# Splitting layer 0's score maxima into two halves on GpSimd instead of VectorE

## The chip, the cores and the metric

The kernel runs on one core of a Trainium2 chip. A core has five engines with instruction queues of their own: TensorE (PE; its weight loads are listed as PEld), VectorE (DVE), ScalarE (ACT), GpSimd (POOL) and SyncE (SP), which issues transfers. Each queue is worked off in its fixed order, and engines wait for each other by semaphores. The metric is the device time of one execution in microseconds (us). One profiled execution comes with it, whose span is counted from the first to the last instruction.

## The reference

Two cross-attention layers follow each other, for 8 batches of 100 queries of width 512 and 722 context rows each. Cut to what matters:

```python
# layer 0: 16 heads of width 32
Q = layer_norm(x) @ wq + bq;  K = layer_norm(ctx) @ wk + bk;  V = layer_norm(ctx) @ wv + bv
scores = einsum('bqhd,bkhd->bhqk', Q, K) / sqrt(32)
out = einsum('bhqk,bkhd->bqhd', softmax(scores), V) @ wo + bo
x = x + out
x = x + gelu(layer_norm(x) @ w1 + b1) @ w2 + b2
# layer 1: 16 heads of width 64, on the x of layer 0 and the same context
out = softmax(x @ Wq (x scale) @ (ctx @ Wk).T) @ (ctx @ Wv) @ Wfc + x
out = layer_norm(out) * gamma + beta
```

All inputs and the output are float32.

## The kernel before

Matrix products run on float16 operands. To keep accuracy, every float32 operand is split into a high half (the value rounded to float16) and a low half (the rest, also float16), and a product is made of the three terms of `TERMS`: high x high, high x low, low x high.

The work is cut in 24 units, numbered `u`: units 0 to 7 are the batches of layer 0 with 16 heads each, units 8 to 23 are half batches of layer 1 with 8 heads each. The outer loop at the end of `xattn_kernel` goes over units and heads and calls `step(u, h)`. After each step it takes items from a list (`fill`): projections of keys and values for the next unit, the normalisation and transposition of later context rows (`prep0`, `prep1`), the scaling and splitting of weights (`block`), the feed-forward part (`ffn`), output projections (`post0`, `post1`), each with an estimated cost.

A head of layer 0 goes through these stages.

- `scores`: two matmuls make the 100x722 scores `S` in PSUM, and VectorE reduces them to `nm`, the negated maximum of each of the 100 rows.
- `negated`: `nm` is split into a high and a low half, which are put in columns 96 and 97 of a 100x98 float16 tile, one of a ring of four (`NM`); its other columns are zero. In the high half the value is divided by `MS` = 2048.
- `negated_T`: a matmul with the identity turns that tile, so that the two halves become rows 96 and 97 of a result in the PSUM tile `NZB`, and ScalarE copies them into rows 96 and 97 of the head's queries `q`.
- `front0`: six matmuls make the transposed scores `ST` from 98 rows. Rows 96 and 97 of the keys tile hold the constants `MS` and `LS`, so that the negated maximum is added by the matmul itself. ScalarE takes the exponential into `p` and casts it into the high half of `pt`, and GpSimd makes the low half with two subtractions of 128x300.
- `head_back`: twelve matmuls multiply `pt` with the values into `O`.

`step(u, h)` calls `scores`, `negated` and `negated_T` for head h and then `front0` for an earlier head, of two steps before in layer 0. `S` and `ST` share a PSUM ring of two tiles. In layer 1 `front1` gives `nm` to ScalarE as a bias, and `negated` and `negated_T` aren't called.

The program is not run in the order in which it is written. Each engine's order is laid down by a planner ahead of the run (`TC_KW = dict(schedule_with_timeline_sim=True)`), from estimated durations and priorities; the instructions of a step are raised in priority (`tc.high_priority`). Only in the first steps are the orders of the queues those of the program (`nc.in_order`), with the calls written out by hand in an order of their own. The profile names one line (L40) for nearly all instructions, as they pass through a recording helper (`Engine`), so that groups are told apart by the tiles that they write and read.

The tiles that matter here: `nm` is the maximum and also the split tile, `nzb` the PSUM tile of the turned halves (some projections use it too), `QS` the queries, `S` and `ST` the scores, `p` and `pt` the probabilities, `V` and `KN` the values and keys, `pp` the PSUM tiles of the projections, `nat` a context tile in natural layout, `hl` the two halves of one, `xs` a tile of rows of x.

Of the kernel before, what the change touches and what calls it, by code (L numbers as in the profile page):

```python
# [12 lines left out]
ALU = mybir.AluOpType  # L13
AX = mybir.AxisListType

B, SQ, SK, E, FF = 8, 100, 722, 512, 2048
# [9 lines left out]
MS = 2.0 ** 11  # L26
# [28 lines left out]
def xattn_kernel(  # L55
# [4 lines left out]
    nc = Core(tc)  # L60
# [49 lines left out]
    def ring(name, tiles):  # L110
        i = counters.get(name, 0)
        counters[name] = i + 1
        return tiles[i % len(tiles)]
# [603 lines left out]

    def negated(nm):
        nz = ring("nm", NM)
        nc.vector.tensor_scalar(nz[:, 96:97], nm[:SQ], 1.0 / MS, None, ALU.mult)  # L720
        nc.vector.tensor_scalar(nz[:, 97:98], nz[:, 96:97], -MS, nm[:SQ], ALU.mult, ALU.add)
        return nz

    def negated_T(u, h, nz):
# [732 lines left out]
    def step(u=None, h=None):  # L1457

        with tc.high_priority(offset=80 if u == LAST or u is None and len(pending) and pending[0][0] >= LAST - 1 else 105):
            new = None  # L1460
            if u is not None:
                S, nm = scores(u, h)
                new = (u, h, S, negated(nm) if u < B else nm)
                if u < B:
                    negated_T(u, h, new[3])
            if len(stages) >= (2 if u is not None and u < B else 1):
                v, g, S_, nm_ = stages.pop(0)
                pending.append((v, g, front0(v, g, nm_) if v < B else front1(v, g, S_, nm_)))
                used.add((v, g))
            if new:  # L1470
                stages.append(new)
# [84 lines left out]
```

## Time and profile before

| what | value |
|---|---|
| time, median of 3 runs | 1536.39 us (1535.56 to 1539.84) |
| profiled execution, its own time | 1540.27 us |
| profiled execution, span | 1538.5 us |
| mean granted TensorE clock | 0.966 |
| busy TensorE (matmul) | 1385.8 us, 90% |
| busy VectorE | 1015.8 us, 66% |
| busy ScalarE | 813.6 us, 53% |
| busy GpSimd | 580.4 us, 38% |

Busy shares are averages over stages with different limits: layer 0's heads run in the first 660 us, with the preparation of all weights beside them, and layer 1's from then on. A line of the waits view reads: engine and tile that waited, the engine and tile that ended the wait, total us, number of waits, longest. A line of the groups view reads: engine, operation, out<-in, partitions x elements and type, count, busy us, mean ns of one, then the idle time of the engine ahead of them and what ended it.

### The profile page before, as it was taken

To read this page: it belongs to the slowest core of one execution; us is meant where nothing else is said; L and a number is where in the kernel's file an instruction comes from. 1 tells how busy PE (TensorE), PEld (TensorE's weight loads), DVE (VectorE), ACT (ScalarE), POOL (GpSimd) and SP (SyncE) were. 2 spreads that over 40 slices of the span, in tenths; PEclk is the share of its full clock that TensorE was granted. 3 is DMA by queue.
4 is the path that set the end of the run, shared out by engine and by line. 5 is a ranking of instruction groups with operands and counts; after the bars stand their busy time and mean duration, and the time that the engine had idled before them with its cause. 6 is when DMAs were issued, how large, how long until landed. Compare 5 with 4: busy or idle time off the path is not lost. (4 is left out here: it accounts for less than half of the span.)

```text
span 1538.5 us, 33710 instructions
## 1 busy us (share of the span) xinstructions
PE 1385.8 (90%) x12586; PEld 985.0 (64%) x12586; DVE 1015.8 (66%) x2744; ACT 813.6 (53%) x1552; POOL 580.4 (38%) x572
## 2 busy tenths in 40 slices
PE   6888888897878999898999898999899999999996
PEld 5666666676657775566666566666566676566674
DVE  7787888888895676675456755556854555545555
ACT  4455767788865776654354343444343444334442
POOL 4145565665674453452123232122322222323341
PEclk9899999899979999999999999999999999999998
DMA  8567899998966565579577879687768867867684
GB/s 214 131 144 189 211 240 220 238 235 223 239 153 175 164 195 185 132 173 195 144 174 198 173 173 212 160 181 188 176 156 206 187 162 189 185 158 152 149 170 111
DMA packets 456660, 279.20 MB, mean 181 GB/s; under 512 B 348932, under 2 KB 387892, under 8 KB 456496
## 3 DMA queue, kind: packets, MB, share of 16 engines
q1 hardware_dynamic: 454352, 277.02, 74.3%
q8 instruction: 99, 1.62, 0.4%
q14 instruction: 65, 0.53, 0.1%
q10 hardware_dynamic: 2112, 0.01, 0.1%
q0 software_dynamic: 32, 0.01, 0.0%
HBM read 150.88 MB, written 35.30 MB: 121 GB/s over the span
## 5 line engine op out<-in xcount | busy, mean ns | idle before, releaser
L40 POOL TENSOR_TENSOR stage<-p,stage 100x722 f16<-100x722 f32 x124 | 194.1, 1570 | 477.1 <-DVE stage L40 242.3
L40 PE MATMUL pp<-wres,ctxT 128*128 128x256 f16 (+3 forms) x2004 | 335.3, 320 | 8.7 <-DVE KN L40 5.4
L40 PE MATMUL pp<-ctxT,wres 128*128 128x361 f16 x1836 | 326.2, 327 | 17.0 <-DVE V L40 6.3
L40 PEld LDWEIGHTS <-wres 128*128 128x128 f16 x2496 | 240.4, 100 | 144.3 <-issue 22.0
L40 PEld LDWEIGHTS <-ctxT 128*128 128x128 f16 (+1 forms) x2376 | 238.4, 103 | 141.7 <-issue 15.4
L40 DVE TENSOR_REDUCE nm<-S 100x1 f32<-100x722 f32 x256 | 229.9, 900 | 62.0 <-PE S L40 60.3
L40 POOL TENSOR_TENSOR pt<-p,pt 128x300 f16<-128x300 f32 x256 | 200.0, 804 | 180.2 <-ACT pt L40 100.1
L40 PE MATMUL O<-V,pt 128*128 128x64 f16 (+5 forms) x3840 | 201.5, 191 | 27.1 <-DMA pt<-stage 8.2
L40 PEld LDWEIGHTS <-pt 128*128 128x128 f16 (+1 forms) x3840 | 173.7, 99 | 69.2 <-issue 10.2
L40 PE MATMUL S<-ks,QS 128*100 128x361 f16 (+1 forms) x768 | 175.3, 327 | 26.1 <-DVE nm L40 10.8
L40 ACT ACTIVATE p<-S,nb,sig 100x722 f32<-100x722 f32 x128 | 121.8, 953 | 116.3 <-DVE nb L40 99.0
L40 DVE TENSOR_TENSOR V<-pp,V 128x256 f16<-128x256 f32 (+2 forms) x196 | 90.6, 463 | 106.9 <-ACT V L40 106.6
L40 ACT CAST V<-pp 128x256 f16<-128x256 f32 (+2 forms) x196 | 79.2, 407 | 152.7 <-PE pp L40 97.0
L40 PEld LDWEIGHTS <-QS 128*100 128x100 f16 (+1 forms) x768 | 88.5, 127 | 49.4 <-issue 23.6
L40 PEld LDWEIGHTS <-wst 128*128 128x128 f16 x1152 | 100.2, 99 | 13.8 <-DMA wst<-W1S 2.8
L40 ACT ACTIVATE p<-ST,sig 128x600 f32<-128x600 f32 x128 | 97.1, 758 | 13.8 <-PE ST L40 10.0
L40 ACT CAST KN<-pp 128x361 f16<-128x361 f32 x89 | 40.9, 460 | 104.1 <-PE pp L40 92.0
L40 ACT CAST pt<-p 128x600 f16<-128x600 f32 x128 | 88.1, 689 | 2.1
L40 DVE TENSOR_TENSOR KN<-pp,KN 128x361 f16<-128x361 f32 x89 | 47.2, 531 | 56.3 <-ACT KN L40 54.8
L40 PE MATMUL nzb<-ctxT,wres 128*128 128x361 f16 x468 | 81.7, 318 | 2.1 <-DVE sx L40 1.3
L40 PE MATMUL nzb<-wres,ctxT 128*128 128x512 f16 (+2 forms) x372 | 80.6, 366 | 0.2 <-DVE KN L40 0.2
L40 PE MATMUL ST<-QS,ks 98*128 98x100 f16 x768 | 61.0, 212 | 14.7 <-ACT p L40 9.5
(266 smaller groups left out, 2038.9 us busy)
## 6 DMA issues: line engine op xcount, KB each, us to landing
ks<-KN SPq DMA_DIRECT2D x256, 90.2 KB
nat<-in_ctx_dram SPq DMA_DIRECT2D x78, 256.0 KB
ks<-KD SPq DMA_DIRECT2D x96, 180.5 KB
wst<-W1S SPq DMA_DIRECT2D x64, 256.0 KB
wst<-W2S SPq DMA_DIRECT2D x64, 256.0 KB
wst<-WFS SPq DMA_DIRECT2D x48, 256.0 KB
KD<-KN SPq DMA_DIRECT2D x32, 361.0 KB
QS<-QD SPq DMA_DIRECT2D x85, 100.0 KB
```

Of the source, the lines that this page charges most:

```text
L40: r = f(*args, **kwargs)
```

## The change

The two instructions of `negated` are issued on GpSimd instead of VectorE. They are the same operations on the same 100x1 operands; the planner then lays down the orders of all queues anew.

```diff
     def negated(nm):
         nz = ring("nm", NM)
-        nc.vector.tensor_scalar(nz[:, 96:97], nm[:SQ], 1.0 / MS, None, ALU.mult)
-        nc.vector.tensor_scalar(nz[:, 97:98], nz[:, 96:97], -MS, nm[:SQ], ALU.mult, ALU.add)
+        nc.gpsimd.tensor_scalar(nz[:, 96:97], nm[:SQ], 1.0 / MS, None, ALU.mult)
+        nc.gpsimd.tensor_scalar(nz[:, 97:98], nz[:, 96:97], -MS, nm[:SQ], ALU.mult, ALU.add)
         return nz
```

## Prediction

> **What bounds the kernel now.** I read the windows view first, cut at the stretch in which layer 0's heads run (the first score maximum starts at 53.5 us, the last `negated` at 652.8 us). Columns: TensorE, its weight loads, VectorE, ScalarE, GpSimd, then granted clock, DMA share and GB/s.
>
> ```profile
> 55.00:660.00 605.00, 520.97 (x5360) 400.85 (x5359) 466.56 (x1440) 420.36 (x779) 316.79 (x367) 0.94 0.74 194
> ```
>
> TensorE is busy 521 of 605 us and stands still for 84. VectorE has 467 us of work, GpSimd 317, so GpSimd has 288 us free here. From 800 to 1538 us, where layer 1 runs and `negated` is not called, TensorE is busy 695 of 738 us: little to win there, and none of its instructions change. So the question is who ends the 84 us. The waits view of TensorE for the same stretch (us in total, times, longest):
>
> ```profile
> PE S L40 <- DVE nm L40: 10.8, 14, 1.3
> PE ST L40 <- ACT p L40: 9.5, 9, 2.9
> PE pp L40 <- DVE V L40: 7.0, 5, 2.5
> PE O L40 <- ACT pt L40: 6.9, 5, 2.9
> PE pp L40 <- DVE KN L40: 6.6, 7, 2.1
> PE nzb L40 <- DVE nm L40: 6.4, 6, 2.7
> ...
> PE ST L40 <- DVE nm L40: 4.3, 5, 1.5
> PE O L40 <- POOL pt L40: 4.0, 8, 0.8
> ```
>
> All lines that VectorE ends add up to 43.7 us (the five shown 35.1, nine smaller ones 8.6); those of ScalarE 29.8, of GpSimd 4.0. VectorE is thus the most frequent cause, but only half of the idle time. The view of the tile `nm` in this stretch prices what is moved (durations min/median/max in ns):
>
> ```profile
> L40 DVE TENSOR_SCALAR nm<-nm x127: 117/144/157, 56.2 to 652.6; 100x1 f16<-100x1 f32 x127
> L40 DVE TENSOR_SCALAR nm<-nm,nm x127: 177/206/218, 57.4 to 652.8; 100x1 f16<-100x1 f16 x127
> ```
>
> Last, the groups and waits of GpSimd there, which tell what the moved pair will be queued among:
>
> ```profile
> L40 POOL TENSOR_TENSOR pt<-p,pt 128x300 f16<-128x300 f32 x254 | 198.1, 802 | 180.2 <-ACT pt L40 100.1 <-PE nzb L40 22.2 <-PE ST L40 17.8
> ```
>
> GpSimd's main work is the low half of each head's probabilities, two instructions per head, and for 100 us it stands at the head of its queue waiting for ScalarE's cast of that tile (37 times, longest 11.4 us).
>
> **The change part by part.**
>
> *Off VectorE.* 128 heads x (144 + 206 ns) = 44.8 us, 9.6% of VectorE's 467. All that follows a pair in VectorE's queue can be earlier. What TensorE sees of it lies between 0 and 43.7 us (every wait that VectorE ends now). To place it, I took the instruction records: TensorE's gaps of over 0.1 us that end within 0.4 us after a VectorE instruction are 58 and 45.7 us long. From each I walked back through VectorE's queue to its last pause of over 0.12 us, counted the moved instructions in that run and shortened the gap by 175 ns for each, at most by the gap itself. The sum is 19.3 us. Example: the longest, 2.67 us at a `nzb` matmul, follows a run of 18.9 us with 8 moved instructions and shrinks by 1.4. I take 12 of the 19, because ScalarE ends 29.8 us of TensorE's idle time and is late next.
>
> *Onto GpSimd.* 128 x 2 small instructions. No GpSimd TENSOR_SCALAR of this shape is in the trace. Below, a memset of 128x1 takes 98 to 101 ns and one of 100x98 199 ns; above, extending the TENSOR_TENSOR rows to no columns (804 ns at 300, 1570 ns at 722, so 1.8 ns a column) leaves 260 ns, and a per-partition operand may add to it, so I put the upper end at 450 ns. I take 250, next to that intercept, since these instructions read and write as those do. The second one waits for the first: 0.05 us more, an estimate from the gaps of 0.03 to 0.04 us that VectorE shows between the two when nothing stands between. So 128 x 0.55 = 70 us (32 to 122 by the ends), and GpSimd goes from 317 to about 387 of 605 us, still the least loaded of the four.
>
> *Latency of one pair.* Now the pair is done on average 1.77 us after the maximum (0.74 until the first starts, 0.67 between them, because other VectorE work is interleaved, and the two durations). At the end of a maximum GpSimd's running instruction has on average 0.26 us left; with 0.1 to wake up and 0.55 of work the pair would be done after 0.9. TensorE loads `nz` 3.6 us after the maximum in the median (5% of heads under 1.4). Put in at that instant, 3 to 7 of 128 heads would be later than TensorE takes them now, by 1 to 3.4 us together: 2 us.
>
> *What waits behind it.* The new waits are for the maximum (VectorE) and for a free `nz` (TensorE). Queued behind are the `pt` subtractions and the `hl`, `whl` and `xs` work. 19 to 54 GpSimd instructions would be pushed, by 5 to 24 us in all. TensorE's second `O` matmul, first reader of the low half, starts 2.7 us in the median after the subtraction that it needs, under 0.4 us in a tenth of the heads. So about a tenth shows: 1 us.
>
> *What it waits behind.* GpSimd's order is fixed before the run by the planner's estimates. Where a pair stands behind a subtraction whose cast isn't there yet, it waits for work of earlier heads, and `negated_T` then holds TensorE. If every pair stood behind the next GpSimd instruction that hadn't started at the maximum's end, 50 of 128 would be later than now, by 81 us in all (67 to 102 by the ends of the price). I take one in 27, 3 us, since the planner knows both; this is the weakest number here.
>
> *The shared memory port.* The trace shows the two engines excluding each other. VectorE's normalisation, mostly 0.54 us, lasts 2.97 while GpSimd works without a break:
>
> ```profile
> 192.29 2.97 DVE L40 TENSOR_SCALAR nat<-nat,mv,rz 100x512 f32<-100x512 f32 x1
> ```
>
> The 45 of them take 516/540/2973 ns (min/median/max). With GpSimd's load up by 70 us in 605, 12% more of them meet a GpSimd instruction, 45 x 0.12 = 5, by up to 0.25 us each: 1 us, inside the rounding of the terms above. The Trainium skill (Perfetto Trace Analysis, Optimizing Scalar/DVE Operations) speaks against the change: moving work between VectorE and GpSimd may not help because they share a read port. Taken so strictly that GpSimd's new time came back on VectorE in full, it would leave 45 - 70 = -25 us, a loss; the row above shows the lock in full, but only some dozen of the 45 lasted longer than 0.6 us.
>
> *The sum.* -12 + 2 + 1 + 3 = -6 us. The profiled execution took 1540.3 us (span 1538.5 and 1.8 around it), 3.9 over the median of 1536.4, so 1534.3 there and about 1530 as a median. By the bounds: -19 + 1 = -18 at best by the walk, and up to +40 if half of the pairs are queued wrongly and VectorE's gain is nothing.
>
> **The rivals.**
>
> *Slower: pairs queued behind late subtractions.* One mechanism: on GpSimd the pair of head h stands behind the subtraction of head h-2 or h-3, whose cast depends on matmuls that themselves stand behind `nz` of earlier heads. For: the 100 us for which GpSimd waits for that cast, and that VectorE, where the pair stands now, waits for the same kind of thing less (24.8 us for `V`, 15.0 for `KN`). Against: the median slack of 3.6 us. Price 81 us x the share of heads: the 9 us of net gain without it are gone at one head in 9; one in 4 gives +20 - 9 = +11 us, 1547 us; one in 2 gives +31, 1567 us.
>
> *No change: ScalarE takes VectorE's place.* Each 0.35 us freed ends at a wait for ScalarE (420 of 605 us busy, 29.8 us of TensorE's waits now) and the planner's new order gives back the rest: 1536 us, between 1532 and 1541. Against it speaks that VectorE is the busier one, and its `V` and `KN` work is what frees TensorE's `pp` buffers.
>
> *Slower: the price itself.* If the small instructions cost as much as a 300-column subtraction, 0.8 us, GpSimd gets 205 us more and with 522 us is as loaded as TensorE; the pair is done 2.0 us after the maximum instead of 1.77, and subtractions come later by 1.6 us a head, against a slack of 2.7: some 15 us slower, 1551. Nothing in the trace is that slow with so few columns.
>
> **How the numbers follow.** Forecast (faster) 0.45; queueing 0.33; no change 0.18; price 0.04. Changes under 0.3%, 4.6 us, are about what a measurement of this kernel can't tell from none. So faster 0.45, same 0.18, slower 0.37. The faster case by itself runs from 1518 to 1532. The range goes from 1515 to 1560: on the slow side it holds queueing up to some 40% of the heads; the tenth or so beyond it and a few in a hundred below are left out.
>
> **What would show it.** Right: VectorE's busy time from 55 to 660 us lower by 45, GpSimd's higher by 32 to 122; lines in which TensorE waits for VectorE down from 43.7 to about 30; the last `nz` some 6 us sooner; layer 1 of the same length. Wrong in the price: GpSimd's `nm` rows over 450 ns. Wrong in the queue: lines of `nzb` or weight loads waiting for GpSimd's `nm` that reach tens of us, or `O` waiting for GpSimd's `pt` far above 4. Wrong in place: layer 1's length changes by more than layer 0's, which would point to the planner's order and not to the moved instructions.

## The result, and the profile after

The changed kernel takes 1546.22 us (median of 20 runs, 1538.42 to 1555.23), the kernel before 1535.97 in the same comparison (20 runs, 1528.78 to 1548.22). The ratio is 1.0072 (95% interval 1.0056 to 1.0088): slower by about 10 us, where 6 us less were forecast. The mean granted clock of its 20 runs is 0.967; that of the kernel before is 0.966 to 0.967 in the comparisons below.

Executions of one program spread by over one percent, and the profiled ones don't sit at the medians: after's took 1539.1 us, 7 under its median; before's took 1540.3, 4 over. So I profiled both programs a second time (1543.5 and 1528.9 us) and believe only what both pairs show.

Window of the heads of layer 0, first the changed kernel's first profile, then its second, then the second one of the kernel before. Columns as in the prediction: TensorE, weight loads, VectorE, ScalarE, GpSimd, granted clock, DMA share, GB/s.

```profile
55.00:660.00 605.00, 519.91 (x5361) 400.68 (x5359) 444.35 (x1178) 421.79 (x779) 384.46 (x623) 0.94 0.75 194
```

```profile
55.00:660.00 605.00, 522.15 (x5370) 401.10 (x5368) 440.86 (x1180) 421.85 (x779) 385.63 (x623) 0.94 0.74 194
```

```profile
55.00:660.00 605.00, 520.41 (x5413) 402.25 (x5411) 467.37 (x1453) 422.18 (x780) 321.12 (x370) 0.95 0.75 195
```

In this window VectorE has 22 to 26 us less and GpSimd 63 to 69 more; TensorE gets no more done. The pair's 44.8 us don't come off VectorE in full in the whole execution either, where all other instructions are the same in both kernels. Busy time and instructions of each engine, before and after (first profiles):

```profile
PE 1385.8 (90%) x12586; PEld 985.0 (64%) x12586; DVE 1015.8 (66%) x2744; ACT 813.6 (53%) x1552; POOL 580.4 (38%) x572
PE 1383.9 (90%) x12586; PEld 983.7 (64%) x12586; DVE 997.6 (65%) x2488; ACT 814.4 (53%) x1552; POOL 651.4 (42%) x828
```

With the second profiles (1013.2 and 990.6 us) VectorE is busy 20 us less on average, with 256 instructions fewer. Its other instructions took only 2 us longer in all. The rest is overlap: the record of a VectorE instruction often begins before the one ahead of it has ended. Two rows of the kernel before, of which the first ends at 192.24 and the second begins at 192.17, while the next (192.29, shown in the prediction) begins before 192.37:

```profile
192.10 0.14 DVE L40 TENSOR_TENSOR rt<-rt,ra 128x3 f32<-128x3 f32 x1
192.17 0.20 DVE L40 TENSOR_SCALAR nm<-nm,nm 100x1 f16<-100x1 f16 x1
```

Of the pair's 45 us of records in the kernel before only 17.4 us lie where no other VectorE instruction runs, 68 ns an instruction. VectorE was relieved of about 20 us, not of 45. The view of the tile `nm` prices the moved pair (min/median/max in ns):

```profile
L40 POOL TENSOR_SCALAR nm<-nm x128: 202/213/1350, 55.1 to 651.7; 100x1 f16<-100x1 f32 x128
L40 POOL TENSOR_SCALAR nm<-nm,nm x128: 269/270/1880, 55.4 to 652.0; 100x1 f16<-100x1 f16 x128
```

TensorE's waits in the same window (us in total, times, longest), lines of the changed kernel:

```profile
PE pp L40 <- DVE KN L40: 11.7, 11, 3.7
PE nzb L40 <- ACT QS L40: 8.0, 9, 2.3
PE S L40 <- DVE nm L40: 7.7, 8, 2.4
PE O L40 <- POOL pt L40: 5.7, 12, 0.9
PE O L40 <- DVE On L40: 5.4, 4, 4.3
...
PE ST L40 <- DVE nm L40: 4.8, 5, 1.6
PE nzb L40 <- POOL nm L40: 4.3, 4, 2.5
```

Added up by what ended them, both profiles of each kernel (before / before again, after / after again):

| TensorE waits for, us | before | after |
|---|---|---|
| VectorE, `nm` | 23.6 / 23.9 | 12.5 / 8.0 |
| VectorE, `KN` | 6.6 / 6.1 | 11.7 / 12.3 |
| VectorE, `On` | 1.4 / 1.4 | 5.4 / 5.4 |
| VectorE, all | 43.7 / 42.4 | 42.3 / 39.0 |
| ScalarE, all | 29.8 / 31.6 | 23.6 / 22.9 |
| GpSimd, all | 4.0 / 4.2 | 10.0 / 11.0 |
| DMA, all | 4.4 / 4.7 | 6.9 / 8.6 |
| all | 81.9 / 82.9 | 82.8 / 81.5 |

So 13.5 us of waits for `nm` do vanish (means: 23.75 to 10.25), and all of it comes back in this window under other names. What is lost in time is not one line. Counted by work, the start of the maximum of head 152, at which TensorE has issued 6950 matmuls in each of these four profiles, stands at 840.0 and 832.9 us before, at 841.7 and 842.1 after: 5.5 us later by the means. From there to the start of the last maximum nothing differs beyond what two executions of one kernel do: 670.4 and 666.0 us before, 667.7 and 671.5 after.

GpSimd's waits in the changed kernel, and a piece of its timeline (start, duration, instruction), show the pair's new surroundings:

```profile
POOL pt L40 <- ACT pt L40: 78.8, 47, 11.6
POOL nm L40 <- DVE nm L40: 44.2, 32, 4.6
```

```profile
265.80 0.21 POOL L40 TENSOR_SCALAR nm<-nm 100x1 f16<-100x1 f32 x1
265.97 1.65 POOL L40 TENSOR_TENSOR pt<-p,pt 128x300 f16<-128x300 f32 x2
267.58 1.15 POOL L40 TENSOR_TENSOR hl<-nat,hl 100x512 f16<-100x512 f32 x1
268.69 1.15 POOL L40 TENSOR_TENSOR whl<-stage,whl 128x512 f16<-128x512 f32 x1
269.94 0.27 POOL L40 TENSOR_SCALAR nm<-nm,nm 100x1 f16<-100x1 f16 x1
```

The planner has put four instructions, 4 us of work, between the two halves of one pair. Something stands between the two in 54 of the 128 heads; on VectorE it did in 91, but what stood there was shorter. From the instruction records, the pair is done 2.49 us after the maximum on average (1.77 before): 0.97 until the first starts, 0.92 between the two (0.67 before), the rest their own time. And a head's first subtraction now starts 0.86 us after the cast that it needs instead of 0.50, 46 us over 128 heads.

### The profile page after: what moved, and what is told of

Read it like the earlier page. It is cut to its first block, busy times and chain, and to the rows that moved or that the text cites. A ratio compares the mean times of both kernels' runs of the same rounds, so it can differ in the third digit from the quotient of the medians.

```text
span 1537.3 us, 33699 instructions
## 1 busy us (share of the span) xinstructions
PE 1383.9 (90%) x12586; PEld 983.7 (64%) x12586; DVE 997.6 (65%) x2488; ACT 814.4 (53%) x1552; POOL 651.4 (42%) x828
## 5 line engine op out<-in xcount | busy, mean ns | idle before, releaser
L40 POOL TENSOR_TENSOR pt<-p,pt 128x300 f16<-128x300 f32 x256 | 196.6, 789 | 81.1 <-ACT pt L40 78.8
L40 PEld LDWEIGHTS <-QS 128*100 128x100 f16 (+1 forms) x768 | 86.5, 127 | 42.0 <-issue 16.3
L40 DVE CAST stage<-p 100x722 f16<-100x722 f32 x64 | 36.6, 572 | 56.1 <-ACT p L40 51.4
```

The lines of the kernel that those rows point to most:

```text
L40: r = f(*args, **kwargs)
```

## The experiments

The theory that lay nearest was the rival of the prediction: GpSimd's queue, with the pair late in it or the subtractions pushed by it. Against it stood the lines above, in which `nzb` waits for GpSimd's `nm` only 4 us. It is called theory A below. Theory B: the planner lays down another order, and what it lays down is worth some 10 us either way, whoever does the pair. That the orders differ is shown: with the pair left out, the sequences of all five engines differ between the two kernels, while two executions of one kernel have the same.

All ratios are to the unchanged kernel in the same comparison. Where two experiments are set against each other, the quotient of their ratios is mine, with the half-widths added in quadrature as a rough interval.

**Both kernels again.** No edit.

> The changed kernel once more, for a second profile and a second measure of its loss (11 us, ratio 1.0072; its first profiled execution took 1539.1 us, 7 under its own median). Theory A (GpSimd's queue: subtractions stand behind pairs and pairs behind late work): ratio 1.005 to 1.009, and in the profile head 64 starts over 8 us later than in the profile of before, with most of the loss gone into layer 0. Theory B (the planner's new order as such, with no link to GpSimd): the same ratio, with the loss anywhere, layer 1 included.

> The kernel before against itself: ratio 1.000, with an interval that shows how small a difference five rounds can tell, some 0.2 to 0.3%. A second profile shows how much the time of one head moves from execution to execution: under 3 us if the profiles can be compared head by head, 10 us if they can't.

Measured: after again 1542.70 us, 1.0050 (1.0027 to 1.0073); before again 1531.65, 0.9988 (0.9964 to 1.0012). The loss is real and lies between 0.3 and 0.9%; the second profiles are the ones used above. The sign that was set for theory A, head 64 over 8 us later, is there (12 us by the means), but it tells nothing: TensorE has issued 2909 matmuls by then instead of 2824, so the new order has put other work ahead of that head.

**Load without the move, and the move without the relief.** The pair is computed twice; nobody reads the copy `nd`, a ring of four 100x2 tiles.

```diff
         nc.vector.tensor_scalar(nz[:, 97:98], nz[:, 96:97], -MS, nm[:SQ], ALU.mult, ALU.add)
+        nd = ring("nd", ND)
+        nc.gpsimd.tensor_scalar(nd[:, 0:1], nm[:SQ], 1.0 / MS, None, ALU.mult)
+        nc.gpsimd.tensor_scalar(nd[:, 1:2], nd[:, 0:1], -MS, nm[:SQ], ALU.mult, ALU.add)
```

The second of the two kernels has it the other way round: pair on GpSimd, copy on VectorE.

> VectorE makes the pair as before; GpSimd makes the same two instructions as well, into a tile that nobody reads. So GpSimd has the load of the changed kernel and its waits for the maximum, but TensorE waits for nothing of it, and VectorE isn't relieved. Theory A in the form that subtractions are pushed and GpSimd stands waiting for maxima: the loss is here as well, 8 to 15 us over before. Theory A in the form that the pair itself comes late: no loss, within 4 us. Theory B: any value within 10 us of before, of either sign.

> GpSimd makes the pair as in the changed kernel; VectorE makes the same two instructions as well, into a tile that nobody reads. So VectorE's relief of 45 us is taken back, all else stays. My prediction put 12 us on that relief: this run should then be some 12 us slower than the changed kernel, ratio to before about 1.015. If the relief is worth nothing, the ratio stays at 1.005 to 1.009. Theory B: within 10 us of the changed kernel, of either sign.

Measured: copy on GpSimd 1540.79 us, 1.0040 (1.0017 to 1.0062); pair on GpSimd and copy on VectorE 1548.24, 1.0089 (1.0055 to 1.0124). Read at face value, the load alone would be 6 us, and giving VectorE its work back costs 1.0089 / 1.0050, 0.4% (about 0.4 either side), 6 us where the prediction had 12 for the relief. The first of the two lies between the forecasts for the two forms of theory A (8 to 15 us, and within 4). But each kernel has an order of its own, and the next two sets show what that is worth.

**Other orders for both kernels.** Three edits that change nothing that a head computes, each made in the kernel before and in the changed one: a fifth tile in the ring of `nm`, and other priorities of a step.

```diff
-    NM = [const.tile([SQ, 98], F16, name=f"nm_{i}") for i in range(4)]
+    NM = [const.tile([SQ, 98], F16, name=f"nm_{i}") for i in range(5)]
```

> The kernel before with a ring of five split tiles (`NM`) instead of four: the same instructions on the same engines, but the planner sees one wait less and lays the queues down a little differently. It measures what a new order alone is worth. Theory A (the loss comes from the pair on GpSimd): ratio to before 0.997 to 1.003. Theory B (any new order moves the time by as much as the change did): a ratio that is off by 0.5% or more, of either sign.

> The changed kernel with the same ring of five. Theory A: slower than e5 by 7 to 12 us, as the changed kernel is slower than the one before (ratio to before about 1.006). Theory B: its distance from e5 can be anything from -8 to +8 us. If the pair on GpSimd were late for want of a free tile, the fifth would take some of the loss away, 3 us or more.

```diff
-        with tc.high_priority(offset=80 if u == LAST or u is None and len(pending) and pending[0][0] >= LAST - 1 else 105):
+        with tc.high_priority(offset=80 if u == LAST or u is None and len(pending) and pending[0][0] >= LAST - 1 else 110):
```

> The kernel before with the priority offset of a step at 110 instead of 105 for the planner: the same instructions on the same engines in a largely new order. Theory A: within 0.3% of before, or off by some amount that e8 shares. Theory B: off by 0.5% or more, of either sign, and not shared.

> The changed kernel with the priority offset of a step at 110. Theory A: slower than e7 by 5 to 12 us. Theory B: anything from -8 to +8 us against e7.

| kernel | before with it | after with it | after : before |
|---|---|---|---|
| as it was (result) | 1535.97 us | 1546.22 us, 1.0072 | 1.0072 ± 0.0016 |
| five `nm` tiles | 1538.93 us, 1.0014 (0.9991 to 1.0037) | 1551.24 us, 1.0102 (1.0074 to 1.0130) | 1.0088 ± 0.0036 |
| priority 110 | 1540.86 us, 1.0010 (0.9987 to 1.0034) | 1538.18 us, 1.0012 (0.9988 to 1.0035) | 1.0002 ± 0.0033 |

A fifth tile doesn't help, so nothing speaks for a missing free tile as the cause. Neither edit moves the kernel before by an amount clear of the noise, against theory B's forecast of 0.5% or more. With priority 110 the loss is gone, although the pair is nearly as late as in the changed kernel (2.39 us after the maximum) and the subtractions are too (0.93 us after the cast), and `nzb` waits for GpSimd's `nm` for 6.6 us instead of 4.3. So the two latencies that the queueing theory needs don't decide the time by themselves; theory A forecast 5 to 12 us here.

**One half of the maximum.** Only the high half is computed, so the low half of the maximum stays zero; on VectorE, then on GpSimd.

```diff
         nc.vector.tensor_scalar(nz[:, 96:97], nm[:SQ], 1.0 / MS, None, ALU.mult)
-        nc.vector.tensor_scalar(nz[:, 97:98], nz[:, 96:97], -MS, nm[:SQ], ALU.mult, ALU.add)
```

> VectorE makes only the high half of the negated maximum; the low half stays zero (a shift of all scores of a row by the same amount cancels in the softmax). GpSimd has no part in it. VectorE is relieved of 128 x 206 ns = 26 us, against 45 us in the changed kernel. My prediction's term (12 us of gain for 45 us) gives 7 us: ratio to before 0.9955. If relief of VectorE gives nothing by itself because the planner's new order and ScalarE take it back: ratio 0.998 to 1.002. Theory B (any new order moves the time): anything from 0.994 to 1.006.

> The changed kernel with only the high half, on GpSimd: one small instruction per head there instead of two, VectorE relieved of the full 45 us. Theory A (GpSimd's queue): the cost goes with the number of small instructions, so about half of the loss is left while the relief stays whole: ratio to before 0.998 to 1.003, some 5 us or more faster than the changed kernel. If the cost is the extra hop through GpSimd's queue whatever the number of instructions: 1.005 to 1.008 as in the changed kernel.

Measured: on VectorE 1534.45 us, 1.0002 (0.9975 to 1.0029); on GpSimd 1537.52, 1.0023 (0.9999 to 1.0046). Leaving out 128 instructions of 206 ns (26 us by their records) with no other engine involved brings nothing that can be measured, but it isn't the test of 26 us that it was meant to be: VectorE's busy time is 1006.2 us, 8 less than the mean of the two profiles of before. On GpSimd, with one instruction that nothing can split, it is done 1.03 us after the maximum, and it is no gain either. Here VectorE's busy time is 1012.4 us, only 2 less, though both instructions of the pair are gone from it: its other instructions took 23 us longer in all, of which those that read a PSUM tile took 0.7.

**Half of the subtractions.** GpSimd's second subtraction per head is left out (and its part of the tile cleared once), so the low half of half the probabilities is zero.

```diff
-        for c in range(0, 6, 3):
+        for c in range(0, 3, 3):
             nc.gpsimd.tensor_tensor(
                 pt[:, 6 + c : 6 + c + 3, :SQ], P[:, c : c + 3], pt[:, c : c + 3, :SQ], ALU.subtract)
```

> The kernel before with the second of the two GpSimd subtractions per head of layer 0 left out (half of the low parts of the probabilities stay zero): GpSimd has about 100 us less to do. It is the base for e12. GpSimd isn't what bounds the kernel before (4 us of TensorE's waits): ratio to before 0.997 to 1.001.

> The changed kernel with the same subtraction left out: GpSimd has the pair, and still some 35 us less to do than in the kernel before. Theory A (GpSimd's load, subtractions pushed back by pairs): the loss goes, and what is left is VectorE's relief, e12 equal to e11 or up to 8 us faster. If the loss is in the pair's own lateness or in the planner's order: e12 stays 6 to 12 us slower than e11.

Measured: pair on VectorE 1530.15 us, 0.9969 (0.9948 to 0.9991); pair on GpSimd 1522.78, 0.9928 (0.9899 to 0.9957). Against each other 0.9959 ± 0.0036: here the move gains 6 to 7 us, as theory A had it, and as much as was forecast for the full kernel. The window of the second shows why it is tempting to call this the proof of the queueing theory:

```profile
55.00:660.00 605.00, 531.57 (x5486) 408.17 (x5484) 436.14 (x1219) 427.59 (x796) 292.94 (x503) 0.95 0.76 198
```

GpSimd has 92 us less to do than in the changed kernel, and TensorE gets 125 more matmuls into the window. But TensorE still waits for the pair, longer than in the changed kernel:

```profile
PE nzb L40 <- POOL nm L40: 6.4, 13, 1.0
```

The next two experiments ask again, from the other side.

**Load doubled, and the pair put first.** In one kernel GpSimd computes the pair and also the unread copy `nd`; in the other the pair is raised above everything else of its step.

```diff
-                new = (u, h, S, negated(nm) if u < B else nm)
+                if u < B:
+                    with tc.high_priority(offset=300):
+                        nm = negated(nm)
+                new = (u, h, S, nm)
```

> The changed kernel with the pair made twice on GpSimd, the second time into a tile that nobody reads: GpSimd's load rises by as much again as by the change (62 us). Theory A (GpSimd's load: its subtractions, that TensorE needs, are pushed back and pairs wait among them): about twice the cost, 8 to 15 us over the changed kernel, ratio to before 1.011 to 1.016. If the loss came from the pair's lateness alone or from the planner's order: within 5 us of the changed kernel.

> The changed kernel with the pair raised further in priority for the planner (300 above its step), so that it stands ahead of subtractions wherever both are ready. GpSimd's load is the same. If the loss is the pair standing behind subtractions: half of it or more goes, ratio to before under 1.004. If it is the subtractions being pushed: no better, 1.005 to 1.009, or worse.

Measured: two pairs on GpSimd 1543.87 us, 1.0061 (1.0042 to 1.0079), no more than the changed kernel with one, though GpSimd has 64 us more to do in the window (448 against 384). The doubled cost that theory A forecast (1.011 to 1.016) isn't there; as this kernel too has an order of its own, a smaller price of the load isn't excluded. The pair put first: 1536.74, 1.0016 (0.9996 to 1.0036), two thirds to three quarters of the loss gone (against 1.0050 and 1.0072). That is what was set down as the sign of pairs standing behind subtractions. Its waits show what became of `nzb` and the subtractions:

```profile
PE O L40 <- POOL pt L40: 4.9, 11, 1.2
PE nzb L40 <- POOL nm L40: 0.8, 2, 0.7
```

TensorE waits for the pair 3.5 us less than in the changed kernel. The averages barely move (pair done after 2.37 us, subtraction 0.80 after its cast), and the sum of all its waits in the window is 82.0 us against 82.8. What it regained, 5 to 9 us, isn't in the lines of GpSimd alone, and a new order that happens to be a better one would look the same: this run doesn't tell the two apart.

**One subtraction of double width.** GpSimd makes the low half in one 128x600 instruction, in both kernels.

```diff
-        for c in range(0, 6, 3):
-            nc.gpsimd.tensor_tensor(
-                pt[:, 6 + c : 6 + c + 3, :SQ], P[:, c : c + 3], pt[:, c : c + 3, :SQ], ALU.subtract)
+        nc.gpsimd.tensor_tensor(pt[:, 6:12, :SQ], P, pt[:, 0:6, :SQ], ALU.subtract)
```

> The kernel before with the two subtractions of 128x300 in one of 128x600: the same result with 128 GpSimd instructions fewer, some 1.34 us (by the rows: 260 ns and 1.8 ns a column) instead of 2 x 0.756, 22 us in all; the first half of the low part comes later by some 0.6 us. GpSimd isn't what binds the kernel before: ratio 0.998 to 1.003. It is the base for e16.

> The changed kernel with the merged subtraction; nothing is left out. GpSimd's load is 40 us over before instead of 62. Theory A (load): the loss against e15 is smaller than the changed kernel's 10 us, at 3 to 7 us. If the planner's order decides: any value.

Measured: with the pair on VectorE 1556.12 us, 1.0131 (1.0112 to 1.0150); on GpSimd 1549.81, 1.0096 (1.0066 to 1.0126). The kernel with less work for GpSimd (281 us in the window instead of 317) is 20 us slower, where no change was forecast. That the first half of the low part comes later in one wide instruction could be part of it, but TensorE's `O` waits for GpSimd's `pt` for 2.5 us here and for 4.0 in the kernel before. Between the two kernels the move now gains, just at the edge of the noise: 0.9965 ± 0.0036.

**A third order for both.** Priority 100 in place of 105, the same line as above.

> The kernel before with the priority offset of a step at 100, a third order besides 105 and 110: base for e18. Both theories: within 0.5% of before.

> The changed kernel with the offset at 100. If the pair on GpSimd costs by itself (its lateness, 2.5 us after the maximum in place of 1.8, and subtractions 0.36 us later): slower than e17 by 5 us or more. If the loss is that of the orders drawn at 105: between -5 and +5 us against e17, as e8 against e7 (-1 us).

Measured: before 1556.22 us, 1.0117 (1.0096 to 1.0137); after 1541.88, 1.0025 (1.0003 to 1.0047). Against each other 0.9909 ± 0.003: with this order the same move gains 14 us. Both forecasts missed: the base was to stay within 0.5% of before, and theory B's range for the move ended at -5 us. The windows, first the pair on VectorE, then on GpSimd:

```profile
55.00:660.00 605.00, 515.67 (x5231) 395.20 (x5230) 461.84 (x1400) 411.59 (x759) 305.41 (x358) 0.92 0.73 190
```

```profile
55.00:660.00 605.00, 516.56 (x5323) 396.32 (x5320) 440.80 (x1166) 415.24 (x771) 384.85 (x619) 0.95 0.76 193
```

TensorE is busy equally long in both and makes 92 more matmuls in the second: the clock was granted at 0.95 instead of 0.92. TensorE's waits are the same here (87.6 and 86.5 us), although in the faster kernel it waits for GpSimd's pair for more than twice the 4.3 us of the changed kernel:

```profile
PE nzb L40 <- POOL nm L40: 9.6, 10, 4.2
```

**What the runs say together.** Six pairs of kernels differ in nothing but the engine of the pair: 1.0072, 1.0088, 1.0002, 0.9909, 0.9965, 0.9959. Their mean is 0.9999 and their standard deviation 0.007, a standard error of 0.003; a 95% interval from six values is 0.7% wide to either side. Priorities and the fifth tile, which leave every instruction of the unchanged kernel as it was, move it by 0.10, 0.14 and 1.17%, of which only the last is clear of the noise. Theory A's forecasts came true, or nearly, with the fifth tile, the high half on GpSimd, half of the subtractions and the pair put first, and failed with both other priorities, two pairs and the wide subtraction. So what is shown: one and the same move is worth from -0.9 to +0.9%, with the order that is laid down around it, and the sign found in the order at issue doesn't hold in all others. Its mean can't be told from zero, nor from the 0.4% of gain that were forecast.

No kernel here that does all of the work beats the kernel before. Its four other orders (five tiles, both priorities, wide subtraction) stand at 1.0010 to 1.0131, 1.0068 on average, and the five of the changed kernel at 1.0012 to 1.0102, 1.0061 on average. So the 0.72% may well compare a good order of the one kernel with an ordinary one of the other; no run tells what would make it good.

What the order changes was sought in the 20 profiles. A fit over them gives the span as 1344.6 us + 1.05 x TensorE's idle time + 0.32 x the time at half clock, with 2.0 us left over (standard deviation). Idle time is the span minus TensorE's busy time from the page; the time at half clock comes from the trace's record of the granted clock. As the span is busy plus idle time in any case, what the fit adds is that TensorE's busy time grows by 0.32 us for each us at half clock. Some of them:

| profile | span, us | TensorE idle | half clock |
|---|---|---|---|
| before / before again | 1538.5 / 1527.1 | 152.7 / 149.0 | 106.9 / 88.6 |
| after / after again | 1537.3 / 1541.7 | 153.4 / 155.1 | 93.9 / 100.6 |
| pair put first | 1535.3 | 149.8 | 110.3 |
| half of the subtractions, before / after | 1529.2 / 1521.0 | 147.5 / 141.0 | 101.1 / 87.4 |
| priority 100, before / after | 1551.2 / 1543.1 | 162.4 / 162.4 | 119.4 / 83.0 |
| one wide subtraction, before / after | 1549.2 / 1549.6 | 157.8 / 157.2 | 125.1 / 121.3 |

In the change at issue half clock is equal (97.8 and 97.3 us by the means), and the clock of all its runs is that of before. Its profiles differ by 6.7 us (1532.8 to 1539.5 by the means) where the medians differ by 10. Of the 6.7, 3.4 are idle time, which is less than the two executions of the kernel before differ by (152.7 and 149.0), and 3.3 are busy time that the fit doesn't account for. With priority 100 it is the clock: idle time is equal, and the changed kernel runs 36 us less at half clock, 12 us by the fit, where the profiles differ by 8 and the medians by 14.

**What stays open.** Which feature of the new order costs the 10 us isn't settled; no single queue position was shown to. Only some 3 of them are seen as idle time, another 3 as longer busy time of TensorE without a cause, and the last 3 to 4 aren't in the profiles at all. An experiment that moves the pair and keeps every other queue as it was wasn't tried, so the cost of the move in the old order is not known.

## Why the prediction was wrong, point by point

- *The price* was right: 213 and 270 ns in the median against 250 each (277 and 327 in the mean, since some take up to 1.9 us). 128 x 0.60 = 77 us by the means, 68 in the net of the window (316.8 to 384.5), against 70. The time between the two where nothing stands between is 0.10 us, against 0.05. The rival with 0.8 us is out.
- *The relief*, the largest term, was mis-sized from its start. "128 heads x (144 + 206 ns) = 44.8 us" adds up records that overlap with their neighbours and sets the sum against a busy time that counts overlap once; what came off VectorE's busy time is 20 us (22 to 26 in the window, where 45 was named as the sign of being right). The walk shortened gaps by 175 ns for each moved instruction where it stands alone for 68 on average; with 68 the 19 us become about 10 (an estimate from the walk made again over the same trace) and the 12 taken about 6, and the sum -6 + 2 + 1 + 3 is nothing. TensorE's waits for VectorE's `nm` did fall by 13.5. But the lines that VectorE ends were to go from 43.7 to about 30 and are at 42.3 and 39.0: `KN` took 5.7 of it (means of the two profiles), `On` 4.0.
- **The step that failed** is the sum itself, "-12 + 2 + 1 + 3 = -6 us". It shortens gaps of the old order one by one and lets everything else stand. The walk through VectorE's queue found what each gap could shrink by; what came next on every queue was not that of the old trace. It puts nothing for the planner's new order. In its place the runs show waits of 82 us with and without the change, and one and the same move that is worth from -14 to +14 us by the order around it, as much as the largest term in the sum. What in this order makes the 10 us stays open. Among its signs of being wrong the prediction named the order ("Wrong in place"), and expected it in layer 1's length; the loss lies before head 152. The high half alone on VectorE fits this: 8 us less of VectorE's busy time, nothing moved to another engine, and nothing gained.
- *The latency of the pair* was mis-sized: 0.9 us after the maximum was forecast, 2.49 measured. The time to the first instruction, 0.97 instead of 0.36, and the time between the two, 0.92 instead of 0.05, are what was missed; the second because the records of VectorE showed 0.67 between the two there and I took it for a habit of that queue and not of the planner.
- *What waits behind it* was mis-sized as well: 5 to 24 us of pushed subtractions were forecast, 46 measured. TensorE's line for it, `O` waiting for GpSimd's `pt`, rose from 4.0 and 4.2 to 5.7 and 6.5: 2 us, against the 1 taken. So both latencies were too small by a factor of two or more and cost little in TensorE's waits.
- *The queueing rival* gave 1547 us at one head in four, close to the 1546 measured, but its signs aren't there. The first was to be `nzb` waits of "tens of us"; they are 4.3 and 4.5. The second was `O` waiting for GpSimd's `pt` far above 4; it is 5.7 and 6.5. With priority 110 the `nzb` waits are 6.6 and the loss is gone, with priority 100 they are 9.6 and the change gains 14 us.
- *The rival of no change* had the right mechanism in one half-sentence ("the planner's new order gives back the rest") and the wrong engine: ScalarE's lines fell, from about 31 to 23 us. Its range ended at 1541.
- *The shared port* was looked for in the wrong rows. The normalisation of the context tiles is unchanged in its median, and its longest is shorter. Tile `nat` in the window:

```profile
L40 DVE TENSOR_SCALAR nat<-nat,mv,rz x45: 532/541/1469, 75.8 to 463.8; 128x512 f32<-128x512 f32 x32, 82x512 f32<-82x512 f32 x7, 100x512 f32<-100x512 f32 x6
```

It was 516/540/2973 in the first execution of the kernel before and 529/540/1376 in the second, so the 2.97 us were those of one execution, and GpSimd's 68 us more don't show here. They show in the moved instructions themselves. 35 of the 256 last over 60 ns longer than their median, and beside 34 of these VectorE ran an element-wise instruction of 0.38 us or more that reads no PSUM tile; beside the other 221 it did in 23 cases. The second profile has the same numbers but for 21 in place of 23. An example from the changed kernel, where the median is 0.21 us:

```profile
151.49 1.45 DVE L40 TENSOR_SCALAR nat<-nat,mv,rz 128x512 f32<-128x512 f32 x3
151.66 1.35 POOL L40 TENSOR_SCALAR nm<-nm 100x1 f16<-100x1 f32 x1 [2.78 <-PE pp L40]
```

In all the moved instructions are 15.5 us longer than their medians would make them. The prediction put 1 us for the port, on VectorE alone. The warning of the Trainium skill (Perfetto Trace Analysis, Optimizing Scalar/DVE Operations), that the two share a read port and a move between them might not help, agrees with these rows; that the port made the 10 us isn't shown, as the moved instructions take 74 us by their records with priority 100 too, where the move gains, and 75 with priority 110, where it costs nothing.

## What to carry to other kernels

Where a planner lays the queues, an edit of one instruction is an edit of all orders: measure first what edits that mean nothing do to the time (here up to 1.2%), and take a local sum smaller than that for no forecast of sign. Price what is taken off an engine by how much less its busy time would be, not by the durations of the records, which overlap. To learn what a move is worth, make it under several orders and compare within each; one pair of kernels tells about that pair. And a wait that disappears by name is a gain only if the sum of the waits falls: add them all up, in two executions.

## What was not expected of the hardware

The granted clock falls to half in the middle of a busy kernel. The records of the 20 profiles have 15 to 27 such stretches each, nearly all of 3.4 us or a multiple of it, 83 to 125 us in all. Within layer 0's window, TensorE stood still in the 3.4 us ahead of each stretch for at least 1.1 us, 1.9 to 2.3 in the median, where an average piece of that length has 0.4 to 0.5. Not every such pause is followed by one: in the changed kernel 14% of the 177 pieces are idle for over 1.2 us, and there are 14 stretches. Cut on the grid of the clock's own records (all 20 profiles, 7917 pieces of 3.4 us at full clock from 55 to 1500 us), no piece that was idle for under 1.1 us was followed by half clock and each one idle for over 2.03 us was; of those idle for 1.4 to 1.6 us 21% were. The Trainium skill (TensorE: Matmul & The Clock Gate, HAM oscillation — how this bites in real kernels) puts the limit at idle gaps of about 3.4 us, a whole window; here pieces that were a third to two thirds idle came ahead of the drop. By the fit above 3.4 us at half clock cost 1.1 us. That an order which bunches its idle pays for it a second time is what this suggests; no run set only the bunching apart. The executions of one program differ in it too: 106.9 and 88.6 us of half clock in two of the kernel before.

Second, by the records of one column the two engines are close: GpSimd takes 213 and 270 ns for what VectorE does in 144 and 206, 133 ns more per head. In busy time they aren't. Without the pair VectorE would be busy 17.4 us less in the kernel before, GpSimd 73.4 us less in the changed kernel: 0.14 us a head against 0.57.
